# The experts' last weights centered once in DRAM, and a last layernorm without its mean

## The chip, the cores and the metric

The kernel runs on one core of a Trainium2 chip. The metric is device time in microseconds (us) of one execution. The profile is one profiled execution of the same program; its span runs from the first instruction to the last.

## What is computed

Two layers on x of 8 batches, 256 channels, 32 x 32 positions, that is 1024 tokens a batch (the rest of the kernel's source calls a half of a batch, 512 tokens, a chunk; there are 16). Layer 0 is a Mamba block (a scan over tokens with 512 inner channels and 16 states) and a feed-forward block, each with a layernorm and a residual. Layer 1 is an attention over 8 heads and then a mixture of experts: each batch is routed to two of eight experts. The part that the change touches is the end of the experts:

```python
h = jax.nn.gelu(jnp.einsum('nd,edf->enf', xf, W1) + b1[:, None, :], approximate=False)
y = jnp.einsum('enf,efd->end', h, W2) + b2[:, None, :]
...
out = jnp.einsum('ne,end->nd', w_dense, y).reshape(B, S, D)
out = _layer_norm(out + x, gamma, beta)
```

Here x is itself the output of a layernorm without gain, so its mean over the 256 channels is zero. W2 is [8 experts x 512, 256] (eW2 in the kernel, float32, 4 MB), b2 is eb2.

## The kernel before

All tiles hold channels on the 128 partitions and tokens along the free axis; 256 channels are two halves (KC = 2), so a chunk is a tile of 128 x 1024 float32 (512 KB). 25 such buffers (t4) are shared by everything; four more hold scan inputs (h4), four hold attention scores after exp (pt).

The program is recorded by one loop over scan steps (16 chunks x 32 steps of two channel blocks and one state). A step is, on VectorE (DVE): `inputs` (hb = xd * B, 128x1024), two `scan` instructions (128x512 each), and `sums` (hb = hb * C); ScalarE (ACT) makes the factors da = exp(dt * A) two steps ahead (`decay`, line 587; four da buffers, freed by the scans); POOL issues a DMA that adds hb onto the accumulator dx in SBUF; SP loads the rows B and C of a state, broadcast over partitions (`bc`, `load_bc`, line 574, two states ahead, three buffers).

Everything else is written as Python generators ("streams") that are recorded in between. `Model` and `Queue` (lines 62 to 121) keep a modelled time for each engine; a stream yields the time at which its next part may be recorded, or POLL when it lacks a buffer or a bank. `advance` (line 1565) walks modelled time up to where DVE is, in ticks of 0.15, and at each tick runs the streams that are due in the order of urgency: attention, `prologue` of the next chunk (started at step FRONT = 8), `gate_part` (started at step GATE = 17) and `epilogue`, output projection, setup, and last the experts and their `finish`. Streams below the first three urgencies hold back while PE or ACT is more than LAG = 8 ahead. Where PE has nothing, `keep_warm` (line 1551) records a product with zeros ("warm", or "num" inside an open attention sum). So the order of every engine's instructions is fixed when the kernel is built, by these modelled costs and due times; on the chip each engine goes through its own in order.

The streams that matter here:

- `prologue(i)`: layernorm, input projection, convolution, dt and the B and C rows of chunk i.
- `gate_part(i)`: loads xn back (xz), eight products z, their evacuation on ACT, Silu; its result sz is used by `epilogue(i)` after the chunk's last step: sz = dx * sz on DVE, mo (output projection), layernorm f, fh, facc, then layernorm t, whose output tn the attention needs.
- `attention(b)`: vp and qkp (projections), then 32 units of four sc products, exp on ACT, four num and four den products; after eight units a group ends with r, h and ot on DVE, and the next group's first num waits for it.
- `experts(b)` (line 1256), and `expert` for the last batch: `route`, six gathers of weight rows from DRAM (indirect DMAs on POOL, two of eW1 and four of eW2), then for each chunk he = xf * W1, gelu, re = he * W2; the first expert's part goes to DRAM (y_d). They start when the attention of that batch is done, so those of batch b run during the scan of batch b + 2.
- `finish(b, c)` (line 1423): two accumulating DMAs add y_d and xf, then the layernorm called y, then beta, the residual t_d and the store. `finish_last` (line 1405) does the same for the last batch with DVE additions in place of DMAs.
- `layernorm` (line 371): mu (two products with mean_w, 1/256), dst = src - mu on DVE (128x1024), Square on ACT, var (eight small products), rsqrt on ACT as exp(-0.5 ln) with one Newton step on DVE, four "pick" products that spread it over partitions, and the multiplication on DVE.

When the scan is over (after step 32 of chunk 15), what is left is: the end of attention of batch 6, `epilogue(15)`, the experts of batch 6, attention of batch 7 and its experts.

Of the kernel before, what the change touches and what calls it, by code (L numbers as in the profile page):

```python
# [17 lines left out]
P = 128  # L18
B, C, L = 8, 256, 1024
KC = C // P  # L20
CH = 512
# [13 lines left out]
E, F = 8, 512  # L35
# [19 lines left out]
def hybrid_kernel(ctx: ExitStack, tc: tile.TileContext, a: dict, out: bass.AP):  # L55
# [6 lines left out]
    class Model:  # L62
# [3 lines left out]
        t = end = moved = 0.0  # L66
# [50 lines left out]
    act, vec = Queue(nc.scalar, act_cost), Queue(nc.vector, vec_cost)  # L117
    pool, pe = Queue(nc.gpsimd, pool_cost), Queue(nc.tensor, pe_cost)
    sp = Queue(nc.sync, lambda *_: 0.1)

    const = ctx.enter_context(tc.tile_pool(name="const", bufs=1))
    dram = ctx.enter_context(tc.tile_pool(name="scratch", bufs=1, space=bass.MemoryType.DRAM))
# [12 lines left out]
    def V(name, i=None, n=1):  # L135
        lo, hi = VEC[name]
        return vecs[:, lo:hi] if i is None else vecs[:, lo + i : lo + i + n]
# [80 lines left out]
    base2 = const.tile([P, NF], F32, name="base2")  # L218

    t_d, xf_d, x1_d = {}, {}, {}  # L220

    psum = ctx.enter_context(tc.tile_pool(name="psum", bufs=1, space=PSUM))

# [23 lines left out]


    T4, H4, PT, AHEAD, LAG, TICK = 25, 4, 4, 2, 8.0, 0.15
    FRONT, GATE = 8, 17  # L250

# [114 lines left out]

    def layernorm(tmp, bank, src, dst, name, gain=None, bias=None, sums=None, stored=None):


        if stored is not None:
            dst = yield from tmp.take(f"{dst}_{name}")
        mu = yield from bank.take(f"mu_{name}")
        for k in range(KC):
            pe.matmul(mu, mean_w, src[:, k, :], start=(k == 0), stop=(k == KC - 1))
        yield
        vec.tensor_tensor(dst, src, mu.unsqueeze(1).to_broadcast([P, KC, CH]), ALU.subtract)  # L380
        bank.put(mu)
        if stored is None:
            yield
            sq = yield from tmp.take(f"sq_{name}")
        else:
            yield max(stored, model.end)
            sq = src
        act.activation(sq, dst, AF.Square)
        yield

        ps = yield from bank.take(f"var_{name}")
        var = ps[:, :P]
        for k in range(KC):
            for q in range(4):
                pe.matmul(
                    var[HD * q : HD * q + HD, :], mean_w[:, :HD], sq[:, k, q * P : q * P + P],
                    start=(k == 0), stop=(k == KC - 1),
                )
        yield

        r, h = sq[:, 0, :P], sq[:, 1, :P]
        act.activation(r, var, AF.Ln, bias=eps_t)
        act.activation(r, r, AF.Exp, scale=-0.5)
        act.activation(h, r, AF.Square)
        yield
        vec.scalar_tensor_tensor(h, var, EPS, h, ALU.add, ALU.mult)
        vec.scalar_tensor_tensor(r, h, -3.0, r, ALU.add, ALU.mult)
        yield

        for q in range(4):  # L410
            pe.matmul(
                ps[:, q * P : q * P + P], pick[:, q : q + 1].to_broadcast([P, P]), r,
                start=True, stop=True,
            )
        yield
        if gain is None and sums is None:
            vec.tensor_tensor(dst, dst, ps.unsqueeze(1).to_broadcast([P, KC, CH]), ALU.mult)
        else:
            for k in range(KC):
                vec.scalar_tensor_tensor(  # L420
                    dst[:, k, :], dst[:, k, :], 1.0 if gain is None else gain[:, k : k + 1], ps,
                    ALU.mult, ALU.mult, accum_out=None if sums is None else sums[:, k, :],
                )
                if bias is not None:
                    vec.tensor_scalar(
                        dst[:, k, :], dst[:, k, :], bias[:, k : k + 1], None, ALU.add
                    )
        bank.put(ps)
        tmp.put(sq)
        return dst  # L430
# [525 lines left out]
    def values_bias(pl):  # L956

        for m in range(KC):
# [6 lines left out]
            yield  # L965
            vec.tensor_tensor(bo2[:, m : m + 1], ps[:, :1], V("bo", m), ALU.add)

    def expert_constants(pl):
        vec.memset(loads_e, 0.0)
        for dst, n, step, mul, add in (  # L970
            (rev_e, E, 1, -1.0, float(E)), (base1, KC, P, 1.0, float(E * C)),
            (base2, NF, P, 1.0, float(E * F)),
        ):
            t = pl.tile([P, n], I32, name=f"ec_{n}", tag=f"s_ec{n}")
            pool.iota(t, pattern=[[step, n]], base=0, channel_multiplier=0 if n == E else 1)
            vec.tensor_copy(dst, t)
            vec.tensor_scalar(dst, dst, mul, add, ALU.mult, ALU.add)
# [278 lines left out]
    def experts(b: int):  # L1256
# [14 lines left out]
        for k in range(2):  # L1271
# [7 lines left out]
                )  # L1279
            for i in range(NF):  # L1280
                pool.indirect_dma_start(
                    out=g2v[:, i, :], out_offset=None, in_=a["eW2"],
                    in_offset=bass.IndirectOffsetOnAxis(ap=rows2[:, k, i : i + 1], axis=0),
                )
            if k == 0:
# [53 lines left out]
    def expert(b: int, k: int, rows1, rows2, w2e, hbias, obias, weights, parts):  # L1339
# [9 lines left out]
            )  # L1349
        for i in range(NF):  # L1350
            pool.indirect_dma_start(
                out=g2v[:, i, :], out_offset=None, in_=a["eW2"],
                in_offset=bass.IndirectOffsetOnAxis(ap=rows2[:, k, i : i + 1], axis=0),
            )
        if k == 0:
# [49 lines left out]
    def finish_last(b, c, r, r2, t, xf):  # L1405

        mem = Owner(t4, 4, 0, 4)
        vec.tensor_tensor(r, r, r2, ALU.add)
        vec.tensor_tensor(r, r, xf, ALU.add)
        yield  # L1410
        mem.put(r2, xf)
        yield from layernorm(mem, banks, r, r, f"y{b}_{c}", V("gamma"))
        for m in range(KC):
            vec.scalar_tensor_tensor(
                r[:, m, :], r[:, m, :], V("beta", m), t[:, m, :], ALU.add, ALU.add
            )
        yield
        mem.put(t)
        yield sp.dma_start(out_v[b, :, :, c * CH : (c + 1) * CH], r)
        mem.put(r)  # L1420
        mem.end()

    def finish(b: int, c: int, r, y):

        mem = Owner(t4, 2, 1, 1)
        tok = slice(c * CH, (c + 1) * CH)
        yield pool.dma_start(out=r, in_=y, accum_op=ALU.add)
        yield pool.dma_start(out=r, in_=xf_d[b][c], accum_op=ALU.add)
        yield from layernorm(mem, banks, r, r, f"y{b}_{c}", V("gamma"))
        yield  # L1430
        for m in range(KC):
            act.activation(r[:, m, :], r[:, m, :], AF.Identity, bias=V("beta", m))
        yield
        yield pool.dma_start(out=r, in_=t_d[b][c], accum_op=ALU.add)
        mem.end()
        t4.put(r, at=sp.dma_start(out_v[b, :, :, tok], r))
# [81 lines left out]
    with tc.tile_pool(name="work", bufs=1) as work_pool:  # L1518
# [99 lines left out]
            pairs.put(*held)  # L1618

        def all_experts():  # L1620
            for b in range(B):
                while not all(("o", b, c) in done for c in range(NCH)):
                    yield POLL
                yield from experts(b)
# [311 lines left out]
```

## Time and profile before

Three timed runs took 3593.7, 3588.51 and 3581.78 us, the median is 3588.51. The profiled execution was timed at 3597.1 us, its span is 3595.3 us, the granted PE clock 0.948 of full speed.

| rows of the profile | count | mean ns |
|---|---|---|
| DVE scan | 1024 | 1210 to 1268 |
| DVE hb multiplication, 128x1024 | 1024 | 1206 to 1220 |
| ACT da, 128x512 | 1024 | 719 |
| PE warm dummy passes | 1296 | 436 |
| ACT dx<-xm, Identity 128x512 | 64 | 710 |
| ACT accumulator read | 16 | 188 |
| DVE t<-vecs,oh, 128x32 and 128x16 | 32 | 183 |
| POOL gathers of expert weights | 96 | 1369 |

How to read the views: the page gives each engine's busy time, then 40 slices with the busy share in tenths, the DMA queues, and the groups of instructions with "busy, mean ns of one | idle time just before them and what ended it". A timeline row is start, duration, engine, line, operation and count, with the idle time before it and its releaser in brackets. A list of waits gives who waited for whom, the sum, how often, and the longest. Most instructions are recorded by one helper and so carry its line, L100; they are told apart by their tiles.

The first scan instruction is at 91.4 us, the last at 3160.31 us. A step of nothing but the scan takes 4.67 us (for instance 278.15 to 282.82). On DVE between 90 and 3160 us the longest sums of waits are 12.4 us (xm for the DMA dt<-u), 11.5 (b_norm for ACT, in setup), 9.5 (hb for POOL state), 8.6 (hb, no releaser seen), 8.3 (sz for the DMA dx<-hb) and 7.6 (s for ACT).

### The profile page before, as it was taken

The numbers are of one execution on the slowest core, as the hardware profiler recorded it, in microseconds if no ns is written. First come the engines' busy times: TensorE is split into PE (matmuls) and PEld (weight loads), VectorE is DVE, ScalarE is ACT, GpSimd is POOL, SyncE is SP. The second block draws the span as 40 slices with busy tenths as digits, with TensorE's granted clock in tenths as the row PEclk, the third lists the DMA queues.
The fourth block names the chain that finished last, engine by engine and source line by source line (L and its number), as shares of the span: only waits on it lengthen the run. The fifth ranks groups of instructions, "written<-read, shape, count | busy, mean of one in ns | idle before, by whom it ended". The sixth has DMA issues, their size and how long they took to land.

```text
span 3595.3 us, 39913 instructions
## 1 busy us (share of the span) xinstructions
PE 3247.4 (90%) x14413; PEld 1434.8 (40%) x14413; DVE 3041.1 (85%) x3322; ACT 2448.8 (68%) x3438; POOL 957.6 (27%) x1052
## 2 busy tenths in 40 slices
PE   7785869998999989999999999999999999999997
PEld 5553444333443334333433334333433343334344
DVE  4979999999989899999999999999999999931021
ACT  3253737686677866787778777887779777853544
POOL 0333123212332124322332234122432233201010
PEclk9877979999899999999999999999999999999999
DMA  4547787778788878888788978897899888921120
GB/s 112 122 101 172 175 175 180 167 180 182 179 186 200 187 164 188 197 195 200 186 202 193 206 177 201 198 206 174 203 209 198 190 185 196 206 69 59 36 77 13
DMA packets 178878, 597.25 MB, mean 166 GB/s; under 512 B 25184, under 2 KB 27872, under 8 KB 178672
## 3 DMA queue, kind: packets, MB, share of 16 engines
q0 software_dynamic: 103392, 364.44, 52.4%
q1 hardware_dynamic: 75280, 230.18, 19.9%
q8 instruction: 115, 1.88, 0.2%
q14 instruction: 91, 0.75, 0.1%
HBM read 234.36 MB, written 58.20 MB: 81 GB/s over the span
## 4 chain that ended last, share of the span: by engine, by line
DVE 39%; PE 28%; issue 12%; ACT 10%; POOL 6%; DMA 5%; another core or an unknown queue 0%; DVEq 0%; POOLq 0%; SPq 0%; ACTq 0%
DVE hb L100 29%; PE re L100 3%; POOL state L100 3%; DVE xm L100 3%; PE he L100 3%; PE warm L100 3%; ACT L100 2%; PE sc L100 2%; PE num L100 2%; POOL g L95 2%; PE fh L100 2%; DMA dx<-hb 2%; PE qkp L100 2%; PE facc L100 2%; PE den L100 1%
## 5 line engine op out<-in xcount | busy, mean ns | idle before, releaser
L100 ACT ACTIVATE da<-dt,neg_a 128x512 f32<-128x512 f32 x1024 | 724.3, 719 | 523.5 <-DVE hb L100 512.6
L95 POOL DMA_DIRECT2D dx<-hb x512 | 443.1, 871 | 1574.9 <-DVE hb L100 1309.0
L100 DVE TENSOR_TENSOR hb<-hb,bc 128x1024 f32<-128x1024 f32 x512 | 624.4, 1220 | 31.4 <-POOL state L100 9.5
L100 DVE TENSOR_TENSOR_SCAN hb<-da,state,hb 128x512 f32<-128x512 f32 x512 | 632.3, 1268 | 2.8 <-ACT da L100 2.6
L100 DVE TENSOR_TENSOR hb<-xm,bc 128x1024 f32<-128x1024 f32 x512 | 617.4, 1206 | 6.8 <-DMA dx<-hb 6.8
L100 DVE TENSOR_TENSOR_SCAN hb<-da,hb 128x512 f32<-128x512 f32 x512 | 603.4, 1210 | 0.1
L100 ACT ACTIVATE pt<-sc 128x1024 f32<-128x1024 f32 x512 | 494.1, 1017 | 96.0 <-PE sc L100 95.0
L100 PE MATMUL warm<-mean_c,zero_c 128*128 128x256 f32 x1296 | 390.8, 436 | 30.7 <-ACT dt L100 8.6
L100 PE MATMUL sc<-qk,qk 32*128 32x512 f32 x2048 | 344.9, 653 | 16.1 <-ACT pt L100 11.7
L100 POOL COPY state<-hb 128x2 f32<-128x2 f32 x256 | 231.7, 905 | 471.1 <-DVE hb L100 462.4
L100 PEld LDWEIGHTS warm<-mean_c,zero_c 128*128 128x128 f32 x1296 | 254.6, 211 | 178.1 <-PE warm L100 52.1
L100 PE MATMUL num<-pt,v 128*32 128x512 f32 x2048 | 279.9, 617 | 25.0 <-DVE ot L100 25.0
L100 PE MATMUL den<-pt,ecb 128*32 128x512 f32 x2048 | 271.8, 600 | 0.0
L100 PE MATMUL facc<-fh,w 128*128 128x512 f32 x512 | 234.1, 603 | 13.5 <-DVE xf_x L100 7.2
L100 PE MATMUL fh<-x_f,w 128*128 128x512 f32 x480 | 227.5, 604 | 6.1 <-ACT fh L100 3.4
L100 ACT ACT_TABLE_LOAD x172 | 220.7, 1283 | 7.8 <-PE var_a L100 4.3
L100 PE MATMUL he<-xe,g 128*128 128x512 f32 x448 | 224.7, 630 | 0.8 <-ACT sz L100 0.3
L100 PE MATMUL re<-he,g 128*128 128x512 f32 x464 | 212.4, 601 | 3.4 <-ACT pt L100 1.5
L100 PEld LDWEIGHTS sc<-qk,qk 32*128 32x128 f32 x2048 | 103.8, 186 | 200.6 <-ACT pt L100 97.9
L100 PE MATMUL mo<-sz,w_out 128*128 128x512 f32 x256 | 124.8, 629 | 53.6 <-DVE sz L100 53.6
L100 DVE SCALAR_TENSOR_TENSOR xm<-xp,vecs,xm 128x512 f32<-128x512 f32 x192 | 143.4, 747 | 14.7 <-ACT xm L100 10.2
L95 POOL DMA_INDIRECT g<-in_eW,rows x96 | 131.4, 1369 | 83.9 <-PE warm L100 28.4
(347 smaller groups left out, 4133.0 us busy)
## 6 DMA issues: line engine op xcount, KB each, us to landing
dx<-hb POOLq DMA_DIRECT2D x512, 512.0 KB
bc<-bc_d SPq DMA_DIRECT2D x256, 512.0 KB
dt<-e POOLq DMA_DIRECT2D x32, 512.0 KB
dt<-u POOLq DMA_DIRECT2D x32, 512.0 KB
xe<-xf_d SPq DMA_DIRECT2D x28, 512.0 KB
xn<-in_x SPq DMA_DIRECT2D x16, 512.0 KB
xn_d<-xn SPq DMA_DIRECT2D x16, 512.0 KB
xz<-xn_d SPq DMA_DIRECT2D x16, 512.0 KB
```

What stands on the lines that cost most here:

```text
L95: f(*args, **kw)
L100: return f(*args, **kw)
```

## The change

A new stream `center` runs ahead of the experts, once. It subtracts from eb2 its mean over the 256 channels (one product, two small subtractions on DVE), and copies eW2 to a new DRAM tensor eW2_d in eight pieces of 128 x 4 x 256: a load on SP into one t4 buffer, four Identity passes on ACT with an accumulator (the row sums), a scaling by -1/256, four Identity passes with that as bias, and a store on SP. The gathers of the last weights in `experts` and `expert` read eW2_d. The layernorm y in `finish` and `finish_last` is called with `centered=True`, which leaves out mu, its two products and the subtraction. GATE goes from 17 to 16. The branch for inputs outside the usual bounds keeps the original eW2 and its own full layernorm; it isn't taken with these inputs.

```diff
+    eW2_d = dram.tile([E * F, C], F32, name="eW2_d", tag="eW2_d")
...
-    FRONT, GATE = 8, 17
+    FRONT, GATE = 8, 16
...
-        mu = yield from bank.take(f"mu_{name}")
-        for k in range(KC):
-            pe.matmul(mu, mean_w, src[:, k, :], start=(k == 0), stop=(k == KC - 1))
-        yield
-        vec.tensor_tensor(dst, src, mu.unsqueeze(1).to_broadcast([P, KC, CH]), ALU.subtract)
-        bank.put(mu)
+        if not centered:
+            mu = yield from bank.take(f"mu_{name}")
+            for k in range(KC):
+                pe.matmul(mu, mean_w, src[:, k, :], start=(k == 0), stop=(k == KC - 1))
+            yield
+            vec.tensor_tensor(dst, src, mu.unsqueeze(1).to_broadcast([P, KC, CH]), ALU.subtract)
+            bank.put(mu)
+            if stored is None:
+                yield
         if stored is None:
-            yield
             sq = yield from tmp.take(f"sq_{name}")
...
+    def center():
+        ps = yield from banks.take("eb2")
+        pe.matmul(ps[:, : KC * E], mean_w, V("eb2"), start=True, stop=True)
+        yield
+        eb2 = V("eb2").rearrange("p (m e) -> p m e", e=E)
+        for m in range(KC):
+            vec.tensor_tensor(
+                eb2, eb2, ps[:, m * E : m * E + E].unsqueeze(1).to_broadcast([P, KC, E]),
+                ALU.subtract,
+            )
+        banks.put(ps)
+        yield
+        mem = Owner(t4, 1)
+        src = a["eW2"].rearrange("(n j p) c -> n p j c", p=P, j=4)
+        dst = eW2_d.rearrange("(n j p) c -> n p j c", p=P, j=4)
+        for n in range(E * F // (4 * P)):
+            t = yield from mem.take(f"eW2_{n}")
+            w = t.rearrange("p a (b n) -> p (a b) n", n=C)
+            yield sp.dma_start(w, src[n])
+            mean = work_pool.tile([P, 4], F32, name=f"eW2_m_{n}", tag="r_rows1", bufs=1)
+            for j in range(4):
+                act.activation(
+                    w[:, j, :], w[:, j, :], AF.Identity, accum_out=mean[:, j : j + 1]
+                )
+            act.activation(mean, mean, AF.Identity, scale=-1.0 / C)
+            for j in range(4):
+                act.activation(w[:, j, :], w[:, j, :], AF.Identity, bias=mean[:, j : j + 1])
+            yield
+            mem.put(t, at=sp.dma_start(dst[n], w))
+        mem.end()
...
-                    out=g2v[:, i, :], out_offset=None, in_=a["eW2"],
+                    out=g2v[:, i, :], out_offset=None, in_=eW2_d,
...
-        yield from layernorm(mem, banks, r, r, f"y{b}_{c}", V("gamma"))
+        yield from layernorm(mem, banks, r, r, f"y{b}_{c}", V("gamma"), centered=True)
...
         def all_experts():
+            yield from center()
             for b in range(B):
```

The built programs show the order on each engine. In the changed one, the 16 subtractions and the 32 products of mu_y are gone; the eight tiles of `center` stand in chunk 0, between the da instructions of its steps, on ACT as "da, da, [tile], da, da, [tile] ..." with one to three pairs of da between tiles, and on SP as load, store, load, bc, store and so on; 31 dummy products fewer are recorded. Counted by chunk on DVE, six chunks (5, 7, 9, 11, 13, 15) have two subtractions less each, and the part after the last scan four less. Before the last scan stand one r, h, ot set and the end of one layernorm x (two multiplications of 128x512, two small ones) that stood after it. On PE, between the last "pick" product of layernorm t of chunk 14 and the first mo of chunk 15 there are five whole units of attention and no group boundary (before: four sc groups with the group boundary and two small groups of var_x among them); after the first mo there are two units' worth of work left of batch 6 (before: six). Three pairs of he of batch 6 stand before vp of batch 7 that stood after it.

More of the change, by code (lines that the diff above doesn't have):

```diff
@@ L367, in hybrid_kernel, with layernorm @@
     banks = Banks(lambda nm, k: psum.tile([P, CH], F32, name=nm, tag=f"bank{k}"), 2)
-    def layernorm(tmp, bank, src, dst, name, gain=None, bias=None, sums=None, stored=None):
+    def layernorm(
+        tmp, bank, src, dst, name, gain=None, bias=None, sums=None, stored=None, centered=False
+    ):
         if stored is not None:
             dst = yield from tmp.take(f"{dst}_{name}")
-        mu = yield from bank.take(f"mu_{name}")
-        for k in range(KC):
-            pe.matmul(mu, mean_w, src[:, k, :], start=(k == 0), stop=(k == KC - 1))
-        yield
-        vec.tensor_tensor(dst, src, mu.unsqueeze(1).to_broadcast([P, KC, CH]), ALU.subtract)
-        bank.put(mu)
+        if not centered:
[7 more added lines that the diff above has]
+                yield
         if stored is None:
-            yield
             sq = yield from tmp.take(f"sq_{name}")
@@ L1351, in expert @@
             pool.indirect_dma_start(
-                out=g2v[:, i, :], out_offset=None, in_=a["eW2"],
+                out=g2v[:, i, :], out_offset=None, in_=eW2_d,
                 in_offset=bass.IndirectOffsetOnAxis(ap=rows2[:, k, i : i + 1], axis=0),
@@ L1428, in finish @@
         yield pool.dma_start(out=r, in_=xf_d[b][c], accum_op=ALU.add)
-        yield from layernorm(mem, banks, r, r, f"y{b}_{c}", V("gamma"))
+        yield from layernorm(mem, banks, r, r, f"y{b}_{c}", V("gamma"), centered=True)
         yield
```

## The prediction

> **What bounds the kernel now.** I read the page first: the engines' busy shares and the 40 slices. VectorE (DVE) is at 9 tenths from slice 5 to slice 34 and nearly idle after that; TensorE (PE) is at 9 almost everywhere, but its 648 "warm" and 153 "num" dummy products (each listed twice, since a float32 matmul runs in two passes) say that its busy share is padded. Then the list of groups, for what a removed instruction costs and what waits for it; then the busy time by stretches of 100 us.
>
> ```profile
> PE 3247.4 (90%) x14413; PEld 1434.8 (40%) x14413; DVE 3041.1 (85%) x3322; ACT 2448.8 (68%) x3438; POOL 957.6 (27%) x1052
> ...
> DVE  4979999999989899999999999999999999931021
> ...
> L100 DVE TENSOR_TENSOR re<-re,mu_y 128x1024 f32<-128x1024 f32 x15 | 18.2, 1215 | 11.2 <-PE mu_y L100 11.2
> ...
> 100.00:200.00 100.00, 76.04 (x430) 49.88 (x428) 93.04 (x123) 34.57 (x50) 35.86 (x39) 0.86 0.53 122
> 200.00:300.00 100.00, 85.89 (x305) 65.04 (x304) 78.89 (x132) 53.73 (x82) 33.07 (x42) 0.77 0.62 130
> ...
> 3300.00:3400.00 100.00, 96.97 (x537) 32.27 (x538) 5.71 (x9) 56.68 (x63) 1.89 (x2) 1.00 0.13 34
> ```
>
> (After each stretch and its length: busy us of PE, weight loads, DVE, ScalarE (ACT), POOL, the clock, DMA share, GB/s.) So there are two regimes. Up to the last scan DVE sets the pace: the wait list of DVE between 90 and 3160 us sums to some 113 us in 3070. From there to 3595.3 PE and the chain through it set it. In the first 300 us ACT is two thirds idle. The end of the first regime and the path into the second are in the timelines of DVE and PE:
>
> ```profile
> 3160.31 1.28 DVE L100 TENSOR_TENSOR_SCAN hb<-da,state,hb 128x512 f32<-128x512 f32 x1
> ...
> 3170.15 1.22 DVE L100 TENSOR_TENSOR sz<-dx,sz 128x1024 f32<-128x1024 f32 x1 [3.36 <-DMA dx<-hb]
> ...
> 3160.45 1.16 PE L100 MATMUL var_t<-fo,pick 128*128 128x128 f32 x8 [1.55 <-DVE fo L100]
> ...
> 3174.79 1.89 PE L100 MATMUL num<-pt,v 128*32 128x512 f32 x8 [4.30 <-DVE ot L100]
> ...
> 3181.24 3.70 PE L100 MATMUL mo<-sz,w_out 128*128 128x512 f32 x8
> ...
> 3208.70 5.42 PE L100 MATMUL fh<-x,w 128*128 128x512 f32 x12
> ...
> 3264.56 3.62 PE L100 MATMUL vp<-wv,tn_t 128*128 128x256 f32 x16
> ```
>
> Here the reader is to see that mo is ready at 3171.37, when sz ends, and starts ten microseconds later, because PE works in order through attention steps of batch 6 that stand before it, one of which waited 4.30 us for ot.
>
> **What the Trainium skill says.** "VectorE: DVE Perf Modes", in its section on the TRN2 errata, gives (N+151)/0.96 ns for a float32 tensor_tensor: 1224 ns at N=1024; the row above has 1215, so it agrees. "ScalarE: Activation LUTs", section "What ACT_TABLE_LOAD costs", gives 280+0.833N ns with a pointer operand and 186+0.833N without, about 93 ns overlapped: at N=512 707, where the da row has 719. "DMA: Bandwidth & Descriptors", section "Anatomy of one DMA", says 2 us fixed plus the bytes at 436 GB/s, 3.2 us for 512 KB; the trace is slower (a 512 KB x<-in_x took 7.75 us on the chain at 337 us), and I use the trace.
>
> **Part by part.** Scan stage first, on DVE's order as the two builds have it.
> - Removed: 12 of the 16 mean subtractions come before the last scan (two each in six of the chunks). One takes 1.11 us from start to start of its successor (3146.46 to 3147.57 for the same shape): 12 x 1.12 = 13.4 us. The wait for mu_y in that stretch, 4.1 us in three places, goes too: no product stands before Square any more.
> - Moved in: one set of r, h, ot (3172.51 to 3174.65, 2.1 us) and the xf end of one layernorm (two of 0.6, two of 0.3) now come before the last scan, because attention of batch 6 is four units further. +4.0.
> - Added on DVE: two 128x16 subtractions, 0.17 each: +0.3.
> - Added on ACT, in chunk 0: eight tiles with eight Identity passes 128x256, four accumulator reads and one small pass. By the skill's formula (no row has the shape) a pass is 0.40 to 0.49, the read is 0.19 by its row: about 4.2 us a tile, 34 us in all, in 300 us in which ACT was idle for 176. They delay da. In ACT's timeline from 137 to 158 us a pair of da is issued every 5.3 us and read two scan steps later: ACT may be held from 144.87 to about 155.6, 10.7 us, before a scan is late. A tile takes 4.2 of it, so its load may be late by 6.5 us when ACT reaches it. I take +4 in all, for one tile beside prologue 1, with bounds 0 and 8 x 3 = 24.
> - Added on SP: eight loads and eight stores of 512 KB. Each store waits for ACT; behind it are bc loads (issued two n ahead, about 18 us, of which some 7 are the transfer) and prologue 1's, whose dt is ready at 257 us for a use at 315. 0. The 8 MB are hidden too: the DMA share is 0.5 to 0.6 there. The POOL gathers read the copy instead of the input, same rows, 0.
> - GATE 17 to 16 moves SP's xz load, eight products of z, ACT's evacuations and two table loads for Silu one scan step (4.67 us) up in every chunk; on SP the xz load now stands ahead of one bc load (0.40 us of issue), POOL gets nothing. Nothing on DVE is added; sz is needed 15 steps later. 0, bounds -10 and +10 (about a tenth of the 113 us of DVE waits, which any new order deals out again).
> Sum: -13.4-4.1+4.0+0.3+4.0 = **-9.2**.
>
> From the last scan to attention of batch 7 (vp). In the changed order five whole units stand between the last pick of var_t14 and mo, no group boundary among them. A unit takes 2.92 us (3191.43 to 3194.35), so mo starts at 3160.45+1.1+14.6 = 3176.1, against 3181.24: -5.1. From mo to fh (27.5 us before): mo 3.6, unit 2.9, mo 3.6, num and den 1.9, so mu_f after 12.0; then wo waits for ot (3.6 after den, as at 3207.73 to 3212.28) and runs 3.4, var_f to fh 5.05: 24.1, so -3.4. fh to mu_t keeps its content: 0. mu_t to vp took 16.2 us (3248.32 to 3264.56) for 8.3 us of products; DVE's routing work comes earlier now, and PE has 9.6 us of work: between 0 and -6, I take -3. Sum **-11.5** (-5 to -17).
>
> Attention of batch 7, PE full: three pairs of he (1.72 each, 3268.02 to 3269.73) are already done and two mu_y pairs are gone: 5 x 1.72 = **-8.6** (-5.2, if one of the two kinds was only filling, to -14, if 13 fewer dummies count).
>
> Last stretch: one mu_y pair of 1.72 in PE's dense run at 3540, and at the end everything between 3572.05 (xf added) and 3575.56 (Square), 3.4 us on the chain: **-5.1** (-3.4 to -6).
>
> Total -9.2-11.5-8.6-5.1 = -34.4, against the profiled span of 3595.3: 3560.9. That run was timed at 3597.1, above the three timed ones; I carry the difference to their median: 3588.5-34.4 = 3554.
>
> **Rivals.**
> 1. *Only what leaves DVE and the last chain counts.* PE's advantage after the last scan is lost to waits (gelu tables, expert gathers): -9.2-5.1, 3574. For it: PE holds fillers wherever its planner saw a gap. Against: mo's ten microseconds behind other work are plain.
> 2. *No difference* (3588): the new order in the eleven steady chunks meets worse waits on DVE and returns 25 to 35 us. For it: the order is planned with modelled times, and some 110 us of waits lie in the main stretch. Against: the counts by chunk hardly differ outside the mu_y rows.
> 3. *Slower: ACT stands at the loads.* ACT is in order; if every tile's load lands over 6.5 us after ACT gets there, da is late and scans stop in chunk 0. The break-even is (34.4+4)/8 = 4.8 us of stall a tile, that is ACT reaching the tile 11.3 us early. At 6.5 us a tile: 3554-4+52 = 3602. For it: a store waiting for ACT stands before the next load on SP. Against: two or more pairs of da stand between the tiles in ACT's order, and loads land in some 7 us.
> That the change doesn't do what it says is ruled out by the order: the 16 subtractions and 32 products are gone.
>
> **The numbers.** Forecast case 0.72, rival 1 0.14, rival 2 0.08, rival 3 0.06. The forecast's own range is 3535 to 3572 (bounds of the tail and GATE); rival 1 carries it to 3578: 3533 to 3578. About 0.3% (10.8 us) is what a measurement can tell from no change: faster 0.86 (forecast and rival 1), within 0.08, slower 0.06.
>
> **What would show it.** The last scan at about 3151 in the profile, with no new "hb <- ACT da" wait of more than 4 us in the first 300 us; mo of the last chunk within 16 us of the last scan; vp about 20 us earlier than 3264.6; no mu_y before Square at the end. Wrong, if the last scan doesn't move, if ACT waits for eW loads and DVE for da, or if the stretch from vp to the end isn't shorter by 8 us or more.

## The result, and the profile after

The changed kernel took 3612.26 us (median of four runs, 3603.2 to 3614.7) against 3589.12 us for the kernel before in the same set: a ratio of 1.0062, with a 95% interval of 1.0037 to 1.0086. It is 0.6% slower, where 3554 was forecast. Its profiled execution was timed at 3603.2 us and has a span of 3601.4 us.

The page of the changed kernel, busy times and DVE's 40 slices:

```profile
PE 3224.0 (90%) x14289; PEld 1404.0 (39%) x14289; DVE 3023.4 (84%) x3308; ACT 2473.5 (69%) x3542; POOL 947.2 (26%) x1052
...
DVE  4978999999989899998999899988999899961021
```

DVE's busy time fell from 3041.1 to 3023.4 us, 17.7 us for 14 instructions less, and the row of re<-re,mu_y is gone: the change does what it says. But among the nines of the slices there are now eights where there were none, from the 19th slice on in about every fourth. So the time went into waits. Here are the busy times over the whole scan stage, from first to last scan of each kernel (stretch, length, then busy us of PE, weight loads, DVE, ACT, POOL, and last the granted PE clock, the DMA share and GB/s), first before, then after:

```profile
91.40:3160.30 3068.90, 2778.67 (x11951) 1213.96 (x11947) 2918.80 (x3078) 2215.63 (x3136) 922.15 (x1000) 0.94 0.81 185
```

```profile
93.80:3201.90 3108.10, 2774.98 (x11960) 1193.11 (x11959) 2910.60 (x3078) 2247.58 (x3251) 911.53 (x1000) 0.94 0.81 185
```

DVE was busy 8.2 us less and idle 47.4 us more (150.1 before, 197.5 after), so the stage is 39.2 us longer; it also begins 2.4 us later. The rest, from the last scan to the end, went from 435.0 to 399.5 us. Together that makes the 6.1 us between the two spans. (The medians differ by 23: the profiled execution of before was timed at 3597.1 us, above its other executions, that of after at 3603.2, below its other three.)

The time from the first scan of a chunk to the first of the next, read from the timeline of DVE, shows where the 39 us lie; chunks 0 to 14, in us:

```
before 228.8 176.2 179.5 183.2 202.7 196.3 201.9 188.9 194.9 187.6 195.0 186.1 196.1 187.5 195.1
after  243.9 176.1 177.0 182.8 202.1 202.6 189.0 198.6 190.5 204.2 188.4 202.2 190.7 202.2 190.3
```

Chunk 0 lost 15.1 us. From chunk 5 on the odd chunks, at whose end a new batch begins, lost 6 to 17 us each, and the even ones gave back about half of it. In the 50 us before a batch's first scan, in chunks 5, 7, 9, 11 and 13 (the columns as above), before:

```profile
1208.20:1258.20 50.00, 47.39 (x312) 19.62 (x310) 44.59 (x49) 41.91 (x60) 11.24 (x13) 0.93 0.91 201
1599.00:1649.00 50.00, 42.43 (x226) 17.53 (x225) 48.64 (x49) 41.00 (x58) 12.16 (x14) 0.97 1.02 224
1981.50:2031.50 50.00, 45.16 (x259) 17.80 (x257) 46.45 (x46) 42.96 (x60) 12.11 (x14) 1.00 1.01 219
2362.70:2412.70 50.00, 45.01 (x249) 17.39 (x248) 46.31 (x47) 42.96 (x60) 11.65 (x14) 0.97 1.00 219
2746.30:2796.30 50.00, 45.22 (x259) 17.83 (x257) 46.55 (x46) 42.98 (x60) 11.93 (x14) 1.00 1.01 218
```

and after:

```profile
1228.40:1278.40 50.00, 43.41 (x294) 16.92 (x297) 36.03 (x40) 36.17 (x51) 9.33 (x11) 0.97 0.73 158
1616.00:1666.00 50.00, 43.84 (x260) 15.94 (x264) 34.37 (x35) 36.15 (x50) 9.52 (x11) 0.90 0.81 179
2010.60:2060.60 50.00, 43.92 (x303) 16.39 (x301) 35.36 (x39) 36.80 (x51) 9.36 (x11) 0.94 0.75 165
2401.20:2451.20 50.00, 44.34 (x260) 16.56 (x264) 32.23 (x31) 35.14 (x47) 8.39 (x10) 0.88 0.77 169
2794.20:2844.20 50.00, 44.04 (x302) 17.08 (x300) 37.42 (x42) 38.10 (x54) 9.48 (x11) 0.92 0.79 174
```

DVE is idle there for 17.5 us in sum before and for 74.6 after. That is 57.1 us more, while its idle time in the whole stage grew by 47.4. What DVE waits for is seen in its timeline, here in one of the five (start, duration, operation, and in brackets the idle time before it with what ended it):

```profile
2423.88 1.23 DVE L100 TENSOR_TENSOR xm<-xm,dt 128x1024 f32<-128x1024 f32 x1 [2.51 <-ACT fo L100]
...
2426.89 1.22 DVE L100 TENSOR_TENSOR tn_t<-tn_t,var_t 128x1024 f32<-128x1024 f32 x1 [1.25 <-PE var_t L100]
2432.49 1.22 DVE L100 TENSOR_TENSOR xf_x<-xr,mu_x 128x1024 f32<-128x1024 f32 x1 [4.39 <-PE mu_x L100]
2440.85 1.23 DVE L100 TENSOR_TENSOR xm<-xm,dt 128x1024 f32<-128x1024 f32 x1 [7.13 <-DMA dt<-u]
```

From 2419.1 to 2441.99 there is no scan. What ends the gap is dt of the next chunk's prologue: the step cannot go on without it, and layernorm t and x fill part of the hole. The waits of DVE from 90 to 3160 us in the changed kernel say the same (who waited for whom: the sum in us, how often, the longest); the sum for dt<-u was 12.4 us in five waits before.

```profile
DVE xm L100 <- DMA dt<-u: 43.8, 9, 7.1
DVE hb L100 <- POOL state L100: 19.1, 6, 8.4
DVE b_norm L100 <- ACT b_nr L100: 13.2, 4, 7.1
```

The rows after the last scan that answer to those shown of before, of DVE and of PE:

```profile
3201.89 1.28 DVE L100 TENSOR_TENSOR_SCAN hb<-da,state,hb 128x512 f32<-128x512 f32 x1
...
3211.59 1.22 DVE L100 TENSOR_TENSOR sz<-dx,sz 128x1024 f32<-128x1024 f32 x1 [3.03 <-DMA dx<-hb]
```

```profile
3221.29 3.70 PE L100 MATMUL mo<-sz,w_out 128*128 128x512 f32 x8
...
3245.90 3.70 PE L100 MATMUL fh<-x,w 128*128 128x512 f32 x8
...
3283.80 1.88 PE L100 MATMUL mu_t<-x,mean_c 128*128 128x512 f32 x4
...
3293.64 3.61 PE L100 MATMUL vp<-wv,tn_t 128*128 128x256 f32 x16
```

Counted from the last scan, vp comes 91.8 us later against 104.3 before.

### The profile page after: what moved, and what is told of

It reads as the page before. It is cut to its first block, busy times and chain, and to the rows that moved or that the text cites. A ratio compares the mean times of both kernels' runs of the same rounds, so it can differ in the third digit from the quotient of the medians.

```text
span 3601.4 us, 39825 instructions
## 1 busy us (share of the span) xinstructions
PE 3224.0 (90%) x14289; PEld 1404.0 (39%) x14289; DVE 3023.4 (84%) x3308; ACT 2473.5 (69%) x3542; POOL 947.2 (26%) x1052
## 5 line engine op out<-in xcount | busy, mean ns | idle before, releaser
L100 PE MATMUL warm<-mean_c,zero_c 128*128 128x256 f32 x1368 | 406.9, 427 | 24.1 <-ACT fo L100 7.0
L100 POOL COPY state<-hb 128x2 f32<-128x2 f32 x256 | 221.7, 866 | 405.4 <-DVE hb L100 393.6
L100 PE MATMUL fh<-x_f,w 128*128 128x512 f32 x480 | 226.8, 604 | 7.0 <-ACT fh L100 3.0
L100 PEld LDWEIGHTS sc<-qk,qk 32*128 32x128 f32 x2048 | 103.3, 187 | 222.0 <-ACT pt L100 120.6
L100 PEld LDWEIGHTS facc<-fh,w 128*128 128x128 f32 x512 | 98.7, 195 | 131.1 <-issue 118.2
```

Of the source, the lines that this page charges most:

```text
L100: return f(*args, **kw)
```

## The experiments

The median of the kernel before was 3589, 3599, 3594 and 3596 us in the four sets of runs, so times are compared within a set, as ratios with their 95% intervals. The last three columns of the tables are in us and come from the one profiled execution of each kernel. Two of these lie far from the median of their kernel: that of e5, at 3561.1 us, 15.6 below it, and that of e11, at 3605.6, 14.7 above it. In the code, "..." marks what is cut, and comments that begin with a run's name are notes.

### First set: the change taken apart

Three edits are in the change: the gate step, the removal of the mean, and the centering. e1 and e2 move the gate alone, in the changed kernel and in the kernel before; e3 has the removal alone, e4 the centering alone.

```diff
-    FRONT, GATE = 8, 16      # e1, from the changed kernel
+    FRONT, GATE = 8, 17
```

> The whole change, with the gate step alone put back from 16 to 17. Of the 41.6 us by which the last scan is late in the changed kernel, some 17 lie in chunk 0 and some 25 in the batches from chunk 7 on. Theory A (the gate step, one scan step earlier, makes the steady loss): the 25 us come back, time about 3586, last scan in the profile at about 3176, chunk 0 still about 244 us long. Theory B (the removed subtractions and products let the planner deal out a worse order): time stays at about 3612, last scan at about 3200. Theory C (the centering at the start makes both losses, by shifting the phase of what comes later): about 3612 too.

```diff
-    FRONT, GATE = 8, 17      # e2, from the kernel before
+    FRONT, GATE = 8, 16
```

> The kernel before with the gate step at 16 and nothing else. Theory A: slower by about 25 us, some 3614, with chunk 0 near its 229 us and every second chunk from chunk 7 on some 10 us longer. Theories B and C: within 8 us of 3589.

```diff
-    FRONT, GATE = 8, 16      # e3, from the changed kernel
+    FRONT, GATE = 8, 17
...
-                    in_=eW2_d,       # e3: both gathers of the last weights
+                    in_=a["eW2"],
...
-            yield from center()
```

> The removal alone: the last layernorm takes no mean and the gate is at 17, but the weights are neither centered nor copied (so the mean over the channels stays in the output). Theories A and C: the gain after the last scan (35 us) and the 13 us of removed subtractions, nothing lost: about 3545, last scan at about 3150. Theory B: the steady loss of 25 us is there: about 3575, last scan at about 3180.

```diff
-    FRONT, GATE = 8, 16      # e4, from the changed kernel
+    FRONT, GATE = 8, 17
...
-        yield from layernorm(..., V("gamma"), centered=True)
+        yield from layernorm(..., V("gamma"))      # e4: in finish and finish_last
```

> The centering alone: the weights are centered and copied at the start and read from the copy, the last layernorm still takes its mean, the gate is at 17. Theories A and B: chunk 0 longer by some 15 us and nothing else: about 3605. Theory C: both losses, about 3630, last scan at about 3202.

| run | median us | ratio | interval | chunk 0 | last scan | from there to the end |
|---|---|---|---|---|---|---|
| before (profile) | | | | 228.8 | 3160.3 | 435.0 |
| after (profile) | 3612.26 | 1.0062 | 1.0037 to 1.0086 | 243.9 | 3201.9 | 399.5 |
| e1 | 3640.35 | 1.0111 | 1.0086 to 1.0135 | 245.9 | 3218.9 | 418.7 |
| e2 | 3623.88 | 1.0069 | 1.0052 to 1.0086 | 226.1 | 3197.3 | 429.8 |
| e3 | 3620.57 | 1.0062 | 1.0045 to 1.0079 | 228.3 | 3199.8 | 415.8 |
| e4 | 3618.79 | 1.0052 | 1.0034 to 1.0070 | 247.6 | 3186.4 | 431.1 |

The expectations weigh three theories: A blames the gate, B the removal, C the centering. Theory A fell at once: with the gate put back the changed kernel is slower still (3640 where 3586 was expected). Yet the gate alone costs the kernel before 0.7%: the same step, 17 to 16, is worth +0.7% in one kernel and -0.5% in the other (1.0111 to 1.0062), so it has no price of its own. The removal alone, 16 instructions of DVE less, is slower too, and worse than theory B had it (3621 us against 3575). The centering alone costs chunk 0 its 19 us and leaves the batches as they were (chunks 9 and 10 of e4 take 188.3 and 194.5 us). C, which laid both losses to the centering, falls with that.

So three unrelated edits, one of which adds nothing and one of which only takes work away, each cost 0.5 to 0.7%. What they share is that each changes the planner's bookings. In e3 part of the missing time is in the same place as in the changed kernel, before the first scan of a batch, but under another name:

```profile
2012.03 1.21 DVE L100 TENSOR_TENSOR hb<-hb,bc 128x1024 f32<-128x1024 f32 x1
2032.06 1.22 DVE L100 TENSOR_TENSOR tn_t<-fo,mu_t 128x1024 f32<-128x1024 f32 x1 [18.82 <-PE mu_t L100]
```

PE was not idle in those 18.8 us; facc, attention units and fillers stood ahead of mu_t. The next batch's first scan comes at 2059.7; the last scan before the wait ended at 2011.

### Second set: the order kept, the instructions taken away

Two theories are weighed here: P lays the loss to the order that the planner deals out, R to the missing instructions themselves, by which the last layernorm ends earlier and its transfers on POOL come ahead of others. e5 makes the removal, with raw weights and the gate at 17, without a change of order: the planner still books the time of the two products and of the subtraction, but nothing is issued. Every queue then has the order of the kernel before, less 32 products and 16 subtractions. e8 was meant as its mirror image: everything is issued, and nothing booked. e6 moves the centering of e4 behind chunk 0; e7 joins e5 and e6.

```diff
-        if not centered:                       # e5, from the changed kernel
+        if not centered or bank is banks:
...
             for k in range(KC):
...
+                if centered:
+                    model.do(pe, pe.cost("matmul", mu, mean_w))
+                else:
+                    pe.matmul(mu, mean_w, src[:, k, :], start=(k == 0), stop=(k == KC - 1))
+            yield
+            if centered:
+                model.do(vec, vec.cost("tensor_tensor", dst))
+            else:
...
```

> The removal alone once more (raw weights, gate at 17, the mean over the channels stays in the output), but the planner still books the time of the mean's two products and of its subtraction, and only issues nothing for them: every queue has the order of the kernel before, less 32 products and 16 subtractions. Theory P (the loss lies in the order that the planner deals out once its bookings change, not in the missing instructions): the scan stage gains its 13 to 18 us, last scan at about 3145, and the tail some 17: about 3557. Theory R (the instructions that are missing make the last layernorm end earlier, and its transfers on POOL's queue come in front of those of the next chunk's dt): the last scan stays near 3200 as in the removal alone, about 3615.

```diff
+            while ("e", 0) not in done:      # e6, from e4
+                yield POLL
             yield from center()
```

> The centering alone (the mean is still taken, gate at 17), but started only when the epilogue of chunk 0 is done. If the 19 us of chunk 0 are local to it (ACT, SP and PE are shared with the setup there): chunk 0 back at 229 us, chunks 1 and 2 longer by less than 5 us, about 3595. Theory P adds that a shifted order may cost 20 to 40 us from chunk 4 on wherever it comes from: then about 3625.

> All of the change, with the mean still booked but not issued, the centering started after chunk 0's epilogue, and the gate at 17. If neither shift costs: 3589 less 13 to 18 in the scan stage less 17 after it, about 3557. Theory P with a cost of the late centering's shift: 3580 to 3600. Theory R: above 3610.

```diff
+        if centered:                            # e8, from e3
+            ps = yield from bank.take(f"var_{name}")
+            for k in range(KC):
+                nc.tensor.matmul(ps, mean_w, src[:, k, :], start=(k == 0), stop=(k == KC - 1))
+            nc.vector.tensor_tensor(
+                dst, src, ps.unsqueeze(1).to_broadcast([P, KC, CH]), ALU.subtract
+            )
...
-        ps = yield from bank.take(f"var_{name}")
+        if not centered:
+            ps = yield from bank.take(f"var_{name}")
```

> The mirror of the removal in the old order: the last layernorm takes its mean as before (products into the bank of its variance, then the subtraction), but the planner books nothing for it; raw weights, gate at 17, output as in the kernel before. So the order is that of the removal alone, with all the instructions of the kernel before. Theory P: as slow as the removal alone (3620) or slower by up to 17 us of instructions in the scan stage and 17 in the tail: 3620 to 3655. Theory R: near the kernel before, 3590 to 3600.

| run | median us | ratio | interval | chunk 0 | last scan | from there to the end |
|---|---|---|---|---|---|---|
| e5 | 3576.75 | 0.9947 | 0.9930 to 0.9965 | 225.0 | 3138.4 | 420.8 |
| e6 | 3624.49 | 1.0079 | 1.0056 to 1.0101 | 226.8 | 3223.2 | 400.1 |
| e7 | 3602.46 | 1.0024 | 1.0015 to 1.0033 | 225.8 | 3211.6 | 390.3 |
| e8 | 3713.42 | 1.0331 | 1.0308 to 1.0355 | 226.4 | 3283.0 | 425.2 |

e5 and e3 issue the same instructions, but for 56 more fillers on PE in e3, which belong to the order that its planner dealt. So they differ in order alone, and in time by 1.0062 to 0.9947, some 41 us. That decides for P: the removal is a gain, and the order that the planner deals out without its bookings costs more than twice as much. R had expected 3615 for e5. In the scan stage of e5 (in its profiled execution, the shortest of six) DVE is busy 13.8 us less than before, and idle 7.3 us less (142.8):

```profile
90.60:3138.40 3047.80, 2746.81 (x11906) 1195.26 (x11900) 2904.97 (x3067) 2213.88 (x3136) 914.23 (x1000) 0.95 0.82 186
```

e6 has chunk 0 back, and pays in the batches (204 to 206 and 193 us for odd and even chunks in turn), as P had warned; e7 has the same pairs. e8 lies far above what P gave it, and it is no clean mirror of e5. Its mean takes the bank of the variance earlier than e3 does, so its order isn't that of e3: from chunk 5 on every queue differs, and the planner books the end of its scans at 3267.4 against 3262.4 us. DVE stands there for unbooked means too (44.6 us in 12 waits for the bank var_y, up to the last scan), and the rest of the 120 us was not taken apart. It decides nothing between P and R.

What the planner books can be read off when the program is built. The loop over scan steps contains a wait of its own: at step 30 of a chunk it books idle time of DVE until dt of the next chunk exists. These bookings, by chunk, and the booked end of the scans and of the program, beside what the runs showed as differences to before (booked times are no chip times; e11 and e12 belong to the third set; e5, e7 to e10 are left out, because there the mean is booked and not issued, or the other way round):

```
idle booked for dt at step 30 of chunks 5, 7, 9, 11, 13 (us)
  before          5.0   0.5   5.0   5.0   5.0
  after          15.0  13.5  13.5  13.5  13.5
  e2 (gate 16)    0.5  24.5  23.0   6.0   4.5
  e3 (removal)   15.0  13.5  29.5  14.5   6.5

           booked: scans end, program end | against before | on the chip: last scan, median
  before           3220.2     3665.1
  after            3253.4     3668.9         +33.2   +3.8       +41.6    +23.1
  e1               3262.7     3700.2         +42.5  +35.1       +58.6    +40.9
  e2               3256.0     3702.2         +35.8  +37.1       +37.0    +24.5
  e3               3262.4     3699.9         +42.2  +34.8       +39.5    +21.1
  e4               3220.5     3665.5          +0.3   +0.4       +26.1    +19.4
  e6               3287.3     3704.0         +67.1  +38.9       +62.9    +30.7
  e11              3226.0     3660.4          +5.8   -4.7       +23.7     -4.7
  e12              3253.0     3668.5         +32.8   +3.4       +31.4     +5.6
```

Where the centering isn't booked into chunk 0 (e2, e3, e6, e12), the booked end of the scans foretells the chip's last scan, as a difference to before, to about 4 us; where it is (after, e1, e4), 8 to 26 us come on top. e11 breaks the rule by 18 us, with a profiled execution 14.7 us above its median. The booked end of the program does less well: it is off the median by 6 to 19 us in the first six changed kernels listed.

The bookings also name the chunks. The longest, 29.5 us in chunk 9 of e3, is where the chip shows the 18.82 us wait. In e2, where 24.5 and 23.0 us are booked in chunks 7 and 9, each of these two lasts 215.1 us on the chip, against 188.9 and 187.6 before. So most of the loss in the batches isn't something that the chip does to the plan. It is in the plan: with other bookings the streams get buffers and banks in another order, the prologue that opens a batch is ready later, and DVE is left without scans.

Over the 42 pairs of FRONT from 4 to 10 and GATE from 14 to 19, the booked end of the kernel before is 3665.1 at its own pair and 3698.0 or more at every other. Over the 70 pairs of FRONT from 4 to 10 and GATE from 12 to 21 with the change it runs from 3660.7 to 3748.4, and its own pair is the second best. The plan of the kernel before stands in a narrow hollow: either constant moved, the removal, or the centering behind chunk 0 leaves it (the centering in chunk 0, e4, does not).

### Third set: the centering without bookings, and another pair

e9 and e10 keep the old order for everything: the mean is booked but not issued, and the centering is issued at fixed scan steps without a booking, in two buffers of pt, idle there. e9 spreads the tiles over steps 4 to 68; e10 crowds them into steps 2 to 37, so that all but the end of the last two tiles falls into chunk 0. e11 and e12 take the removal as the change has it, with the spread centering; e11 has the pair for which the planner books the earliest end, e12 the pair of the change.

```diff
-            yield from center()
...
         for now in range(nsteps):
             i, k = divmod(now, NSTEP)
+            for f in quiet_at.get(now, ()):      # e9 to e12: load, ACT passes or store of a tile
+                f()
```

> All of the change in the order of the kernel before: the gate at 17, the mean booked but not issued, and the centering issued between scan steps 4 to 68 without any booking (a tile every eight steps, in the buffers of pt, which are idle there), so that no queue's order moves except by the added instructions. Theory P (only the order cost the time): the gain of the removal in the old order, some 17 us, less up to 5 us for the centering's 33 us on ACT: 3575, last scan at about 3143. If the centering costs by contention wherever it stands: 3585 to 3595.

> The same with a tile every four scan steps, so that all of the centering falls into chunk 0, as in the change, but again without booking. If the 19 us of chunk 0 come from a moved order there: chunk 0 at about 226 us and 3575. If they come from what the centering takes (ACT's time between two da, the 8 MB on the DMA engines, SP's waits for ACT): chunk 0 at 240 us or more and about 3590.

```diff
-    FRONT, GATE = 8, 16      # e11; e12 keeps 8, 16
+    FRONT, GATE = 7, 19
```

> The removal as the change has it (nothing booked for the mean), the quiet centering over steps 4 to 68, and FRONT and GATE at 7 and 19, the pair for which the planner itself books the least idle time of DVE with the mean gone: its own end of the program is at 3660.4 booked microseconds, against 3665.1 for the kernel before, 3668.9 for the change, 3702.2 for the kernel before with gate 16 and 3699.9 for the removal alone. Over the runs so far the chip stood some 78 us under the booked end. If the bookings explain the loss: 3582, last scan at about 3166. If the agreement so far is chance: anywhere from 3575 to 3625.

> The change with its own FRONT and GATE (8 and 16) and only the centering made quiet (steps 4 to 68). Booked end 3668.5. If chunk 0's loss is gone with it and nothing else moves: 3612 less 17 to 22, about 3592, last scan at about 3183. If the centering costs its time wherever it stands: about 3610.

| run | median us | ratio | interval | chunk 0 | last scan | from there to the end |
|---|---|---|---|---|---|---|
| e9 | 3574.53 | 0.9936 | 0.9916 to 0.9956 | 227.8 | 3146.4 | 424.7 |
| e10 | 3582.42 | 0.9952 | 0.9937 to 0.9968 | 228.2 | 3154.8 | 428.3 |
| e11 | 3590.93 | 0.9983 | 0.9971 to 0.9995 | 234.9 | 3184.0 | 419.8 |
| e12 | 3601.17 | 1.0013 | 1.0003 to 1.0023 | 229.8 | 3191.7 | 402.5 |

e9 computes all that the change computes, in the order of before, and is 0.64% faster than the kernel before: it beats both. e10 does the ACT work of seven of the eight tiles in chunk 0, and loads the last one there; the chunk lasts 228.2 us against 243.9 in the changed kernel. So the time that the centering takes on ACT, SP and the DMA engines need not lengthen the chunk. (The buffers differ as well, t4 in the change and pt in e10; no run separates them from the bookings.)

In chunk 0 DVE is idle for 44.3 us in the changed kernel, 15.8 more than before. Two new waits make that up; e4 has both of them too (8.9 and 8.4 us). The first, on DVE and on PE of the changed kernel:

```profile
102.52 1.22 DVE L100 TENSOR_TENSOR_SCAN hb<-da,hb 128x512 f32<-128x512 f32 x1
111.33 0.69 DVE L100 SCALAR_TENSOR_TENSOR val<-cnt,io_ch 128x512 f32<-128x512 f32 x1 [7.60 <-PE cnt L100]
```

```profile
94.41 15.01 PE L100 MATMUL warm<-mean_c,zero_c 128*128 128x256 f32 x34
109.35 1.95 PE L100 MATMUL cnt<-oh,oh 128*32 128x32 bf16 x64
```

and in e10, on DVE and on PE:

```profile
102.90 1.20 DVE L100 TENSOR_TENSOR hb<-xm,bc 128x1024 f32<-128x1024 f32 x1
104.01 0.69 DVE L100 SCALAR_TENSOR_TENSOR val<-cnt,io_ch 128x512 f32<-128x512 f32 x1
```

```profile
91.62 8.10 PE L100 MATMUL warm<-mean_c,zero_c 128*128 128x256 f32 x36
99.65 1.92 PE L100 MATMUL cnt<-oh,oh 128*32 128x32 bf16 x64
```

In the changed kernel the last oh, cnt's operand, was ready at 100.3, but the fillers ahead of cnt ran to 109.4, and DVE stands at val for 7.6 us. In e10 cnt runs at 99.7, right after its operand, and val waits for nothing. The order is nearly the same here: 17 fillers stand ahead of this cnt in the changed kernel, 18 in e10 and in the kernel before (each gives two records). What differs is how long they take, 15.0, 8.1 and 10.4 us, and with it the granted PE clock. The stretch of these fillers in the changed kernel, before, and in e10 (columns as above; the third number from the end is the clock):

```profile
94.40:109.30 14.90, 14.44 (x35) 7.81 (x35) 9.27 (x11) 5.67 (x16) 1.94 (x2) 0.61 0.33 71
91.40:101.70 10.30, 10.30 (x41) 8.40 (x38) 10.27 (x10) 2.07 (x3) 1.95 (x2) 0.77 0.00 0
91.60:99.60 8.00, 8.00 (x41) 6.75 (x36) 7.86 (x9) 1.44 (x2) 1.10 (x1) 1.00 0.00 0
```

The other two kernels with the centering booked into chunk 0, e1 and e4, have 16.1 and 16.4 us for this group, at clocks of 0.57 and 0.56; the eleven kernels without it have 8.1 to 10.4. What lowered the clock stays open. In these three kernels the first pieces of eW are moved and centered in just this stretch (DMA share 0.33 and 5.67 us of ACT in the changed kernel), while e10 begins its passes on ACT at 119.5 us. So for this half of chunk 0's loss the centering's own work is a rival that no run excludes.

The second wait, at 218 us, is one of order. Eight gathers of attr (204.91 to 217.37 on POOL) stand ahead of the issue of dx<-hb and of a state copy, and hb waits 8.37 us.

```profile
218.64 1.23 DVE L100 TENSOR_TENSOR hb<-hb,bc 128x1024 f32<-128x1024 f32 x1 [8.37 <-POOL state L100]
```

In the kernel before the same eight gathers ran from 194.0 to 205.6, and from 199.8 on DVE worked on cbt, which in the changed kernel comes only behind this hb.

e12 against the changed kernel, 1.0013 against 1.0062, is what booking the centering costs there, about 18 us, and 14 of them are chunk 0's length; the rest of the loss, the odd chunks of 202 to 205 us, stayed. e11 came 9 us above its 3582, and its last scan 18 us behind its 3166, in a profiled execution that was slow for this kernel (there chunk 0 took 7 us more than in e9, and the odd chunks from 7 on 194 to 199, against 185 to 187). By medians it stands at -4.7 us against the kernel before of its set, which is just the booked difference; as the booked end of the program was off by 6 to 19 us elsewhere, that agreement may be luck. Like e9 it is faster than the kernel before and the changed one, though than the first by only 0.17%. The new pair wins back 10 of the 27 us that part e12 from e9, not all of them.

## Why the prediction was wrong

**The step that failed** is the one on waits in the scan stage, which the prediction put at about nothing: "GATE 17 to 16 ... Nothing on DVE is added; sz is needed 15 steps later. 0, bounds -10 and +10", the +4 for the centering, and the 4.1 us of waits for mu_y as a clear gain. It priced instructions and took for granted that the waits of the old order would stay about as they were. The stage was to come out at -9.2 us, with -0.1 of waits in it, and came out at +41.6 (last scan, profile to profile): 8.2 us less of busy time on DVE, 47.4 us more of idle time, and a begin 2.4 us later. In terms of the runs: the gate alone +24 us (e2), the removal's new order about +41 (e3 against e5), the booked centering +19 (e4). They do not add up, as each deals a new order.

By its other points:

- *Instructions of DVE.* Forecast -13.4 + 4.0 + 0.3 = -9.1 us before the last scan; busy time fell by 8.2. Right; and in e5, where nothing is moved or added, it fell by 13.8, for the 13.4. (The prediction's 113 us of DVE waits sum to 120.6 in the list, and to 150.1 as idle time of the stage; only the bounds of the gate rest on that figure.)
- *Centering on ACT.* Forecast about 34 us; its rows in the first 340 us sum to 34.7. By the Trainium skill, "ScalarE: Activation LUTs", section "What ACT_TABLE_LOAD costs", a pass of 256 is estimated at 0.40 us without a pointer operand and 0.49 with one; the rows have 0.401 and 0.522 in the mean, so they agree with the first and nearly with the second.

```profile
L100 ACT ACTIVATE eW<-eW,eW_m 128x256 f32<-128x256 f32 x32 | 14.3, 522 | 0.3
L100 ACT ACTIVATE eW<-eW 128x256 f32<-128x256 f32 x32 | 12.8, 401 | 0.0
L100 ACT ACTIVATION_READ_ACCUMULATOR eW<-eW 128x1 f32 x32 | 6.0, 188 | 0.0
L100 ACT ACTIVATE eW_m<-eW_m 128x4 f32<-128x4 f32 x8 | 1.6, 205 | 0.3
```

- *Rival 1, the advantage after the last scan lost.* Not so: the part after the last scan became 35.5 us shorter, though in part for another reason than the forecast's (below).
- *Rival 2, worse waits in the new order.* That is what happened, and in its size: in chunks 1 to 15 DVE's idle time grew by 31.6 us, where the rival had 25 to 35; chunk 0's 15.8 came on top. The argument against it, that the counts by chunk hardly differ, was no argument: where within a chunk an instruction stands decides, and the list of DVE's waits cannot show how near the old order was to more of them. It had 0.08.
- *Rival 3, ACT standing at the loads.* Refuted as a mechanism: the idle time before these rows (their last column) sums to 0.6 us. That chunk 0's loss (15.1 us, 18.8 in e4) lies inside the bounds of the forecast's term, 0 to 24, is luck, since that term was for late da, and DVE waited for cnt and for state instead.
- *From the last scan to vp.* Forecast -11.5, measured -12.5: mo -1.5 (-5.1), mo to fh -2.9 (-3.4), fh to mu_t -1.7 (0), mu_t to vp -6.4 (-3). The sum is near by luck: two parts are off by more than 3 us, in opposite directions.
- *From vp to the end.* Forecast -13.7, measured -23.0. The last piece, from xf added to the flag, went from 12.8 to 9.4 us, the forecast 3.4. But from the last scan to the end e5 has only -14.2 and e9 -10.3, and e6, which still takes the mean, has -34.9. So more than half of the changed kernel's 35.5 is the long scan stage in another guise: while DVE waits, the other streams get ahead, and less is left for the end. PE's records show it: without the fillers it has 1716 after the last scan before, 1700 in e5, 1616 in the changed kernel and 1584 in e6. The forecast took all of it for a gain.

Not settled: which shortage makes the prologue late in the new orders. The planner's record of it shows polls for a t4 buffer as well as for a PSUM bank in both kernels. Behind the longest bookings (chunk 9 of e3, chunks 7 and 9 of e2) those for t4 sum to 21 to 25 booked us, against 7.5 to 8.4 in the kernel before at the same chunks; in the changed kernel they hardly grew (8.4 to 9.2). No run separates the two.

## What to carry to other kernels

In a kernel whose order is planned when it is built, an edit is priced in two parts: the instructions, and the new order that the changed bookings deal out. The second can be larger and of either sign, so before an edit is judged, run it in the old order (book what you no longer issue, issue what you add without booking it where the engine has room; e8 shows what unbooked work costs on the engine that sets the pace), and only then search for constants again. Where a plan has its own idle bookings, compare them between the two builds first: here they named the chunks, and in four of the five listed builds without the booked centering in chunk 0 the lateness of the last scan to about 4 us, but not the total time. And a shorter tail behind a longer main stage is not a gain until the same tail is seen in an undisturbed order.

## What was not expected of the hardware

- Fillers are not free for what stands behind them, and their price moves with the granted clock. Near the first scans, 34 records of warm passes took 15.0 us in the changed kernel, where the clock was 0.61, and 36 took 8.1 in e10, where it was 1.00; cnt, in order behind them, came 7.6 us late for DVE.
- The loads of eW took 7.6 us from issue to landing and the stores 6.6, by the median of the DMA rows of the first 340 us. The Trainium skill, "DMA: Bandwidth & Descriptors", section "Anatomy of one DMA", gives an estimate of 3.2 us for 512 KB, for DMAs that GpSimd (POOL) issues; these are issued by SP, and took twice that. On POOL x<-in_x, of the same size, took 8.3. It cost nothing visible in e10, which issued all eight loads and six of the stores in chunk 0.
